# A two-phase attention and gated-product kernel: the joint between its phases is re-ordered, the rows before their second norm lose a shift, and a Gram matrix is computed as a triangle

## The chip, the core and the metric

The kernel runs on one core of a Trainium2 chip. The metric is device time in microseconds (us): the median of the runs before is 2426.33 us (three runs, 2426.27 to 2426.43). Four engines compute beside each other, each with its own queue of instructions that it takes in order: TensorE (PE; its weight loads are listed as PEld), VectorE (DVE), ScalarE (ACT) and GpSimd (POOL). SyncE (SP) issues most DMAs, also in order; ACT and POOL issue some.

## The reference, cut to what matters

The input x is 4 x 2048 rows of 512 numbers, all in float32.

```python
x = x + _layernorm(attn(_layernorm(x)))     # attention, causal, one head of 512
x = x + _layernorm(ffn(_layernorm(x)))

def attn(x):
    q, k, v = relu(x @ Wq + bq), relu(x @ Wk + bk), relu(x @ Wv + bv)
    e = q k^T / sqrt(512) - 10000 * causal
    return relu(softmax(e) @ v @ Wo + bo)

def _gated_bottleneck(x2d, conv_w, ...):    # twice, "so" and "si"
    xc = einsum('ngf,gf->ng', x2d.reshape(n, 128, 4), conv_w) + conv_b
    mean, var = over all n = 8192 rows      # one pair for each of 128 features
    xa = gelu((xc - mean) * rsqrt(var + eps) * gamma + beta)
    return xa @ lin_w.T + lin_b             # 512 logits of each row

def ffn(x):
    score_out = softmax(_gated_bottleneck(x, so...))   # the 32 largest of each row are kept
    out_branch = (x @ weight) at these 32 columns, times their scores
    score_in = softmax(_gated_bottleneck(x, si...))    # again the 32 largest
    in_branch = (x at these 32 columns, times their scores) @ weight
    return out_branch + in_branch + bias
```

The mean and variance of the features go over all rows, so no row can pass the second bottleneck before the last row's features exist. That cuts the kernel into two phases.

## The kernel before, in words

Rows are worked on in 16 groups of 512 (`NGRP`, four per sequence), each of four tiles of 128 rows (`TPG`). Phase 1 (`phase1`) computes attention and the features; phase 2 (`phase2`) the gated products. Both exist a second time with `every_key=True`, for inputs whose scores could be too large; whether that second pass runs is decided at the end from a bound (`compare`, L179), and it does not run in what is measured here.

**Phase 1.** `steps` (L906) goes over the groups. For each it does projections and earlier groups' scores as seven products instead of eight (class `Seven`; their PE rows are L555), its own scores (`score_tile`, L673), the maxima over keys, then `fold` (L707, four transposes, PE row L711), `diagonals` (L720: one DVE reduction, L717, and four scalings, L725), `spread` (L727, PE row L730), `weights` (L732: for each key tile a DVE subtraction and an ACT exponential, with row sums on POOL) and the attention products (`attend`, L768, PE row L773). A float32 matmul call shows as two MATMUL rows.

The order on PE, DVE and POOL is written by hand (`tc.manual_schedule`): the order of the calls is the order of the instructions, within each phase. A small planner, `Pace`, does it for DVE: work that DVE has to do is handed over as generators that yield how long each piece takes, `pace.pe(us)` says that PE was given so much work, and the planner emits as many DVE pieces as fit beside it; `pace.flush(job)` emits a job to its end, `pace.drain()` all. The order on ACT and SP in phase 1 is set by the framework, which simulates the program and may mix work of both phases on an engine.

`chain` (L796) is such a job, one for each tile of 128 rows, behind that tile's attention product. `attended` (L782) takes the product out of PSUM on DVE (L788) and through a Relu on ACT (L789). Then `row_norm` (L139) measures the row on DVE (L142, L144, L146), with an inverse square root on POOL (`inv_sqrt`, L137). With m and r, the residual row x is shifted on ACT by -m*r (L806), and DVE forms x1 = a*r + that (L809). x1 is stored, measured by a second `row_norm`, normed (L816) and stored, and DVE forms the features `xg` of both branches: two products with the convolution weights (L222) and two reductions (L824). In groups 0 to 14 further transposes and stores follow; features return by DMA as columns (`fetch_features`, L837), where a DVE statistic of 512 columns (L281) goes into `bn_all`. In the last group `features` (L843) transposes each tile's `xg` on PE (L847) and copies it into `xc` on ACT (L849), and behind the last tile come the two statistics of 512 columns (L851).

**The Gram product.** In the last group there is no next group to project, and its PE time is filled with `bound` (L861): the 512 x 512 product of the query weights with themselves, four blocks of 128 rows (d = 0 to 3), each over four row blocks c, that is 16 calls or 32 MATMUL rows at L869 and, for each d, one ACT Square with a sum (L877). It is a generator too: each `next(filler)` in `steps` emits half a block. Block 0 lies around `A.p7`, block 1 behind `A.p4` and ahead of `fold`, block 2 between `fold` and `spread`, the first half of block 3 ahead of the attention products and its second half at the end, between the features of tiles 1 and 2.

**The joint.** `phase2` (L1137) opens its pools where phase 1's lie; each of its tiles waits for those tiles of phase 1 whose memory it takes. It loads the Gelu table (`warm`, L1154), aggregates the statistics (L1159) to a scale and an offset for each feature (`bn_a2`, `bn_b2`: L1161 to L1170, with one POOL power), loads the weights `wf` by one DMA on SP (L97) and the bias by one on POOL (L90). It transposes the rows of tiles 0 and 1 (L164, copies L165), does half of tile 0's ungated product (`product`, L1311: four calls over c, 512 columns each), then the Gelu of the first 128 columns (`activate`, L1200), tile 0's logits (`logits`, L1223 and L1225), and the product's other half. `xnT` of every tile comes from the pool `wk2`.

**Phase 2's loop** takes one tile of 128 rows per turn: eight MAX8 and eight MATCH_REPLACE8 on DVE for the two branches (L1232, L1240, L1243), exponentials on ACT, masks and sums on POOL, two products on PE. In turn 1 it also does tile 1's ungated product:

```python
if it == 1:
    logits(nxt)
    n.full = product(n.xnT)
```

Of the kernel before, what the change touches and what calls it, by code (L numbers as in the profile page):

```python
# [39 lines left out]
P = 128  # L40
GT = 512
# [12 lines left out]
def sandwich_kernel(ctx: ExitStack, tc: tile.TileContext, io: dict, out: bass.AP):  # L54
# [52 lines left out]
    bn_all = const.tile([P, 2, NGRP, nc.vector.BN_STATS_DIM], F32, name="bn_all")  # L107
# [71 lines left out]
    def compare(ps):  # L179
# [5 lines left out]
        nc.vector.scalar_tensor_tensor(q4, tot[:, 0:1], float(D * D), q4, ALU.mult, ALU.add)  # L185
# [8 lines left out]


    def phase1(every_key):
# [15 lines left out]
        xgp = enter("xgp", TPG)  # L212
# [64 lines left out]
        pace = Pace()  # L277

# [5 lines left out]
        def load(b, g, queues=(nc.sync,)):  # L284
# [3 lines left out]
            n.x, n.ahead = [], []  # L288
# [507 lines left out]
        def chain(n, t):  # L796
# [5 lines left out]
            yield 1.0, (0.55,)  # L802

            shift = sm.tile([P, 1], F32, name="shift")
            combine(shift, m, r, ALU.mult, -1.0)
            nc.scalar.activation(xr, xr, AF.Identity, bias=shift)  # L806
            yield 0.2, 1.2
            x1 = two.tile([P, D], F32, name="x1")
            nc.vector.scalar_tensor_tensor(x1, a, r, xr, ALU.mult, ALU.add)  # L809
# [3 lines left out]
            m, r = row_norm(sm, x1, "x1")  # L813
            yield 1.75, (0.55,)
            xn2 = ap.tile([P, D], F32, name="a")
            nc.vector.tensor_scalar(xn2, x1, m, r, ALU.subtract, ALU.mult)  # L816
            store.dma_start(xn2_d[n.i][t * P : (t + 1) * P, :], xn2)
            yield 0.55, 0.0
            n.xg[t] = xg = xgp.tile([P, 2, P], F32, name="xg")
# [22 lines left out]

        def features(n, t):  # L843
# [4 lines left out]
            for j, br in enumerate(branches):  # L848
                nc.scalar.copy(xc[br][:, t * P : (t + 1) * P], ps[:, j, :])  # L849
                if t == TPG - 1:  # L850
                    nc.vector.bn_stats(bn[br][:, n.i, :], xc[br])  # L851
# [9 lines left out]
        def bound():  # L861
# [4 lines left out]
            for d in range(NC):  # L866
                ps = ps_mm.tile([P, GT], F32, name="mm")
                for c in range(NC):
                    nc.tensor.matmul(  # L869
                        ps, lhsT=w[c][1][:, d * P : (d + 1) * P], rhs=w[c][1], start=(c == 0), stop=(c == NC - 1)  # L870
                    )
                    if c % 2:
                        pace.pe(1.72)
# [3 lines left out]
                nc.scalar.activation(sqr, ps, AF.Square, accum_out=squared[:, 0, d : d + 1])  # L877
# [28 lines left out]
        def steps(n, ahead):  # L906
# [3 lines left out]
            for j in range(NGRP):  # L910
# [129 lines left out]
                if last:  # L1040
                    pace.drain()
                    features(n, 0)
                    features(n, 1)
                    next(filler)
                    features(n, 2)
                    features(n, TPG - 1)
                    break
# [25 lines left out]
        if every_key:  # L1073
            bo = broadcast(wp, "L0_attn_bo")
            for b in range(B):
# [11 lines left out]
                for g in range(GB):  # L1087
# [12 lines left out]
                    for t in range(TPG):  # L1100
# [3 lines left out]
                        if n.i == NGRP - 1:  # L1104
                            features(n, t)
                    if n.i < NGRP - 1:
                        fetch_features(n.i)
                        pace.drain()
        else:
# [24 lines left out]
        p1.close()  # L1134

# [364 lines left out]
```

## Time and profile before

| what | us |
|---|---|
| median of three runs | 2426.33 |
| profiled execution, its own time | 2428.16 |
| its span, first to last instruction | 2426.3 |
| PE busy in the span | 2376.5 (98%) |
| DVE busy | 1791.3 (74%) |
| ACT busy | 1119.3 (46%) |
| POOL busy | 925.5 (38%) |
| last attention product ends (PE) | about 1743.8 |
| first MAX8 of phase 2 starts (DVE) | 1761.35 |

The page gives busy time of each engine, its share in 40 equal slices of the span (a digit is tenths), and the granted TensorE clock. A line of the order of time gives start, duration, engine, line, operation and what it writes and reads; in brackets how long the engine was idle before it and what ended the wait. A line of the waits gives who waited for whom, the total, how often, and the longest. Time of an engine that is not the bound costs nothing by itself.

### The profile page before, as it was taken

The numbers are of one execution on the slowest core, as the hardware profiler recorded it, in microseconds if no ns is written. First come the engines' busy times: TensorE is split into PE (matmuls) and PEld (weight loads), VectorE is DVE, ScalarE is ACT, GpSimd is POOL, SyncE is SP. The second block draws the span as 40 slices with busy tenths as digits, with TensorE's granted clock in tenths as the row PEclk, the third lists the DMA queues.
The fourth block names the chain that finished last, engine by engine and source line by source line (L and its number), as shares of the span: only waits on it lengthen the run. The fifth ranks groups of instructions, "written<-read, shape, count | busy, mean of one in ns | idle before, by whom it ended". The sixth has DMA issues, their size and how long they took to land.

```text
span 2426.3 us, 29523 instructions
## 1 busy us (share of the span) xinstructions
PE 2376.5 (98%) x8418; PEld 1529.0 (63%) x8418; DVE 1791.3 (74%) x3877; ACT 1119.3 (46%) x2352; POOL 925.5 (38%) x875
## 2 busy tenths in 40 slices
PE   8999999999999999999999999999899999999997
PEld 3776858587685858768585776857334444444443
DVE  2587775558866555886655588655599999999997
ACT  2333423233342333334223333322268888888886
POOL 1012210311221031122103112110369999999997
PEclk9999999999999999999999999999999999999999
DMA  6587756567775556876565677633334445444441
GB/s 217 182 238 209 214 163 171 144 182 231 216 205 165 169 142 183 225 223 202 166 171 138 184 216 217 199 114 95 104 85 103 113 113 122 122 113 122 113 122 54
DMA packets 594736, 392.19 MB, mean 162 GB/s; under 512 B 393090, under 2 KB 460162, under 8 KB 594564
## 3 DMA queue, kind: packets, MB, share of 16 engines
q1 hardware_dynamic: 590932, 386.53, 57.8%
q10 hardware_dynamic: 3312, 2.63, 0.4%
q8 instruction: 70, 1.15, 0.2%
q0 software_dynamic: 320, 1.05, 0.1%
q14 instruction: 102, 0.84, 0.1%
HBM read 275.26 MB, written 114.82 MB: 161 GB/s over the span
## 4 chain that ended last, share of the span: by engine, by line
PE 76%; DVE 12%; ACT 4%; issue 4%; POOL 2%; DMA 1%; SPq 0%; POOLq 0%; ACTq 0%
PE acc L555 24%; PE acc L773 19%; PE mm L555 17%; PE mm L673 5%; PE mm L1311 4%; DVE m_si L1232 3%; DVE m_so L1232 2%; PE mm L408 2%; DVE rest_so L1240 2%; DVE rest_si L1240 2%; PE lg L1225 1%; DVE rest_si L1243 1%; DVE rest_so L1243 1%; PE tp L164 1%; PE mm L657 1%
## 5 line engine op out<-in xcount | busy, mean ns | idle before, releaser
L773 PE MATMUL acc<-vo,st 128*128 128x512 f32 x1088 | 475.9, 593 | 0.0
L773 PEld LDWEIGHTS acc<-vo,st 128*128 128x128 f32 x1088 | 205.3, 190 | 239.8 <-issue 234.6
L1311 PE MATMUL mm<-w_L_ffn_weight,xsT 128*128 128x512 f32 x512 | 231.2, 594 | 2.9 <-ACT xsT L165 1.6
L1311 PE MATMUL mm<-w_L_ffn_weight,xnT 128*128 128x512 f32 x512 | 232.2, 596 | 0.0
L137 POOL TENSOR_TENSOR rs_a<-ve_a,neg_half 128x1 f32<-128x1 f32 x64 | 38.4, 600 | 489.1 <-DVE ve_a L146 483.1
L1311 PEld LDWEIGHTS mm<-w_L_ffn_weight,xsT 128*128 128x128 f32 x512 | 97.5, 191 | 125.6 <-issue 115.6
L1311 PEld LDWEIGHTS mm<-w_L_ffn_weight,xnT 128*128 128x128 f32 x512 | 97.9, 192 | 122.6 <-issue 115.4
L137 POOL TENSOR_TENSOR rstd_x<-var_x,neg_half 128x4 f32<-128x4 f32 (+1 forms) x19 | 17.8, 936 | 403.3 <-DVE var_x L310 399.1
L555 PE MATMUL mm<-xnT,wb 128*128 128x256 f32 x720 | 170.1, 379 | 0.0
L555 PE MATMUL acc<-T,wb 128*128 128x256 f32 x720 | 170.1, 379 | 0.0
L743 POOL TENSOR_TENSOR mxsum<-mxsum,st 128x512 f32<-128x512 f32 (+2 forms) x144 | 162.8, 1131 | 14.7 <-ACT st L739 4.3
L555 PE MATMUL acc<-xnT,wb 128*128 128x256 f32 x720 | 165.2, 379 | 0.0
L555 PEld LDWEIGHTS acc<-T,wb 128*128 128x128 f32 x720 | 136.8, 190 | 25.0 <-issue 6.7
L555 PEld LDWEIGHTS acc<-xnT,wb 128*128 128x128 f32 x720 | 136.8, 190 | 25.0 <-issue 6.5
L555 PEld LDWEIGHTS mm<-xnT,wb 128*128 128x128 f32 x720 | 135.3, 190 | 24.0 <-issue 7.2
L673 PE MATMUL mm<-qT,kT 128*128 128x128 f32 (+3 forms) x512 | 148.5, 433 | 0.0
L574 ACT COPY cp<-mm 128x512 f32<-128x512 f32 x72 | 42.2, 586 | 203.6 <-PE mm L555 200.0
L222 DVE SCALAR_TENSOR_TENSOR mxsum<-mxsum,st 128x512 f32<-128x512 f32 (+2 forms) x144 | 86.4, 600 | 65.9 <-ACT st L601 61.3
L1232 DVE MAX8 m_si<-rest_si 128x8 f32<-128x512 f32 x192 | 130.1, 678 | 0.1
L1232 DVE MAX8 m_so<-rest_so 128x8 f32<-128x512 f32 x192 | 128.6, 670 | 0.1
L1240 DVE MATCH_REPLACE8 rest_si<-m_si,rest_si 128x512 f32<-128x512 f32 x192 | 128.5, 669 | 0.0
L1240 DVE MATCH_REPLACE8 rest_so<-m_so,rest_so 128x512 f32<-128x512 f32 x192 | 128.5, 669 | 0.0
(243 smaller groups left out, 4918.5 us busy)
## 6 DMA issues: line engine op xcount, KB each, us to landing
wb<-keys SPq DMA_DIRECT2D x168, 256.0 KB, 3.0
x<-x SPq DMA_DIRECT2D x124, 256.0 KB, 3.0
xr<-in_L_attn_x_dram SPq DMA_DIRECT2D x64, 256.0 KB, 3.6
xn<-xn SPq DMA_DIRECT2D x64, 256.0 KB, 2.8
out_dram<-h SPq DMA_DIRECT2D x64, 256.0 KB, 2.0
xt<-in_L_attn_x_dram SPq DMA_DIRECT2D x62, 256.0 KB, 3.5
wb<-Z_v SPq DMA_DIRECT2D x60, 256.0 KB, 2.9
wb<-Z_q SPq DMA_DIRECT2D x60, 256.0 KB, 3.1
```

What stands on the lines that cost most here:

```text
L137: nc.gpsimd.tensor_tensor(dst, src, neg_half[:, : src.shape[1]], ALU.pow)
L222: nc.vector.scalar_tensor_tensor(out, a, factor, b, ALU.mult, op)
L408: nc.tensor.matmul(ps, lhsT=w[c][1][:, d * P : (d + 1) * P], rhs=xnT[:, c, :], start=(c == 0), stop=(c == NC - 1))
L555: nc.tensor.matmul(ps[:, d * H : (d + 1) * H], lhsT=left[:, c, d * P : (d + 1) * P], rhs=right[:, c, :], start=(new and c + d == 0), stop= ...
L574: nc.scalar.copy(t, ps)
L673: nc.tensor.matmul(ps[:, off:], lhsT=kT[:, c, k : k + P], rhs=n.qT[:, c, off:], start=(c == 0), stop=(c == NC - 1),)
L743: nc.gpsimd.tensor_tensor(n.sum[:, off:], n.sum[:, off:], w, ALU.add)
L773: nc.tensor.matmul(acc, lhsT=n.st[kt][:, t * P : (t + 1) * P], rhs=vos[kt // TPG][:, kt % TPG, :], start=(kt == 0), stop=(kt == nk - 1),)
L1232: nc.vector.max(n.m8[br], n.rest[br] if k else n.lg[br])
L1240: nc.vector.match_replace(n.rest[br], n.m8[br], n.rest[br], -LOWEST)
L1243: nc.vector.match_replace(n.rest[br], n.m8[br], n.lg[br], -LOWEST)
L1311: nc.tensor.matmul(ps, lhsT=lhsT[:, c, :], rhs=wf[:, c, :], start=(c == 0), stop=(c == NC - 1))
```

## The change

Five edits.

1. **Triangle.** Block d of the Gram product takes only columns from d*128 on, so 512, 384, 256 and 128 of them; the planner is told 0.43 us times (4 - d) for half a block, and the bound counts the sum twice.
2. **Rows without the shift.** DVE forms y = a*r + x directly; the shift -m*r is added by ACT afterwards, and only for the row that is stored as x1. The second norm's moments and the normed row are taken from y, whose normed row is the same.
3. **Moments in parts.** In the last group the statistics of `xc` are taken of 384 columns, inside the last chain (`n.early`: one branch behind each `row_norm`), and of the last 128 columns in phase 2, straight from the transposes' PSUM; `bn_all` has one record more.
4. **Order of the joint.** The chains of tiles 0 to 2 are flushed, their features transposed, the Gram's last half emitted, and then the last chain. The last tile's features are transposed in phase 2, behind the whole ungated product of tile 0; aggregates, scale and offset follow there. Tile 1's ungated product lies in halves around tile 0's logits, and is gone from turn 1.
5. **Where tiles lie.** `wf` and `xnT` get pools of their own, next to the bottom of phase 2's memory; the last tile's `xg` gets a pool outside phase 1, and `bn_mv` is among the constants.

```diff
         def chain(n, t):
             m, r = row_norm(sm, a, "a")
             yield 1.0, (0.55,)
+            if n.early:
+                n.early.pop(0)()
+
+            y = two.tile([P, D], F32, name="x1")
+            nc.vector.scalar_tensor_tensor(y, a, r, xr, ALU.mult, ALU.add)
+            yield 0.75, 0.0
             shift = sm.tile([P, 1], F32, name="shift")
             combine(shift, m, r, ALU.mult, -1.0)
-            nc.scalar.activation(xr, xr, AF.Identity, bias=shift)
-            yield 0.2, 1.2
-            x1 = two.tile([P, D], F32, name="x1")
-            nc.vector.scalar_tensor_tensor(x1, a, r, xr, ALU.mult, ALU.add)
+            m, r = row_norm(sm, y, "x1")
+            x1 = xr
+            nc.scalar.activation(x1, y, AF.Identity, bias=shift)
             store = nc.scalar if final else nc.sync
             store.dma_start(x1_d[n.i][t * P : (t + 1) * P, :], x1)
-            m, r = row_norm(sm, x1, "x1")
-            yield 1.75, (0.55,)
+            yield 1.2, (0.55,)
+            if n.early:
+                n.early.pop(0)()
             xn2 = ap.tile([P, D], F32, name="a")
-            nc.vector.tensor_scalar(xn2, x1, m, r, ALU.subtract, ALU.mult)
+            nc.vector.tensor_scalar(xn2, y, m, r, ALU.subtract, ALU.mult)
...
+        def moments_of(br, i, src):
+            nc.vector.bn_stats(bn[br][:, i, :], src)
+
+        def first_moments(n, br):
+            moments_of(br, n.i, xc[br][:, : GT - P])
...
         def bound():
+                cols = slice(d * P, D)
                 for c in range(NC):
                     nc.tensor.matmul(
-                        ps, lhsT=w[c][1][:, d * P : (d + 1) * P], rhs=w[c][1], start=(c == 0), stop=(c == NC - 1)
+                        ps[:, cols],
+                        lhsT=w[c][1][:, d * P : (d + 1) * P],
+                        rhs=w[c][1][:, cols],
+                        start=(c == 0),
+                        stop=(c == NC - 1),
                     )
                     if c % 2:
-                        pace.pe(1.72)
+                        pace.pe(0.43 * (NC - d))
...
                 if last:
+                    pace.flush(*behind[:-1])
+                    for t in range(TPG - 1):
+                        features(n, t)
+                    next(filler)
+                    n.early = [(lambda br=br: first_moments(n, br)) for br in branches]
                     pace.drain()
-                    features(n, 0)
-                    features(n, 1)
-                    next(filler)
-                    features(n, 2)
-                    features(n, TPG - 1)
+                    ends.append(n.xg[TPG - 1])
                     break
...
         wp = enter("wp2", 1)
+        wfp = enter("wf2", 1)
+        xtp = enter("xt2", 3)
...
-        mv = wp.tile([P, 2, nc.vector.BN_AGGR_DIM], F32, name="bnmv")
-        for j, br in enumerate(branches):
-            nc.vector.bn_aggr(mv[:, j, :], bn[br].rearrange("p n s -> p (n s)"))
-        (scale and offset from it)
-        wf = matrix(wp, "L0_ffn_weight")
+        wf = matrix(wfp, "L0_ffn_weight")
...
-        tiles[0].full = product(tiles[0].xnT, part=range(2))
+        tiles[0].full = product(tiles[0].xnT)
+
+        for j, br in enumerate(branches):
+            tp = ps_tp.tile([P, NC, P], F32, name="tp")
+            nc.tensor.transpose(tp[:, j, :], xg[:, j, :], ident)
+            nc.vector.bn_stats(bn[br][:, NGRP, :], tp[:, j, :])
+            nc.vector.bn_aggr(bn_mv[:, j, :], bn[br].rearrange("p n s -> p (n s)"))
+            nc.scalar.copy(xc[br][:, GT - P :], tp[:, j, :])
+        (scale and offset from bn_mv)
+        tiles[1].full = product(tiles[1].xnT, part=range(2))
         activate(xa[0], slice(0, P))
         logits(tiles[0])
-        product(tiles[0].xnT, tiles[0].full, range(2, NC))
+        product(tiles[1].xnT, tiles[1].full, range(2, NC))
         activate(xa[0], slice(P, GT))
...
                 if it == 1:
                     logits(nxt)
-                    n.full = product(n.xnT)
```

## The prediction

> **What bounds the kernel now.** I read the page's busy shares first, then busy time by stage, the chain of waits, the waits around the seam, and the order of time there. On the page:
>
> ```profile
> PE   8999999999999999999999999999899999999997
> DVE  2587775558866555886655588655599999999997
> PEclk9999999999999999999999999999999999999999
> ```
>
> PE is full through phase 1, DVE through phase 2. Busy time in five stretches (stretch, length, then PE, PEld, DVE, ACT, POOL busy, granted clock, DMA share, GB/s) separates the joint from both:
>
> ```profile
> 0.00:1640.00 1640.00, 1629.96 (x6383) 1186.72 (x6384) 1077.30 (x2197) 545.89 (x1074) 288.55 (x324) 1.00 0.66 188
> 1640.00:1693.00 53.00, 53.00 (x220) 40.95 (x219) 22.76 (x48) 10.72 (x24) 0.10 (x1) 1.00 0.38 97
> 1744.00:1761.00 17.00, 10.09 (x27) 4.22 (x25) 9.88 (x24) 7.99 (x20) 2.55 (x7) 0.66 0.86 231
> 1761.00:2403.00 642.00, 624.25 (x1645) 270.63 (x1644) 641.48 (x1531) 532.21 (x1190) 602.91 (x515) 0.99 0.45 109
> ```
>
> Between 1761 and 2403 us DVE idles 0.5 us, so whatever brings its first MAX8 forward brings the end forward by as much. Before 1744 PE does not idle, so there only PE work or a wait that takes its place counts. In the 17 us between, neither is full: latency decides. The chain of waits shows where the Gram product stands in the last group:
>
> ```profile
> 1683.23 3.43 PE mm L869 x8
> 1686.66 0.44 PE tp L711 x4
> 1687.10 3.44 PE mm L869 x8
> 1690.53 0.86 PE mm L730 x2
> ```
>
> and the waits from 1640 to 1760 tell how much later PE came than its consumers:
>
> ```profile
> DVE fold L717 <- PE tp L711: 2.0, 1, 2.0
> DVE st L738 <- PE mm L730: 2.7, 1, 2.7
> ACT pr L877 <- DVE xg L824: 4.3, 1, 4.3
> ```
>
> In order of time, the joint, the last tile's chain and what follows it:
>
> ```profile
> 1743.82 0.75 DVE L788 SCALAR_TENSOR_TENSOR cp<-acc,rsum,r_L_attn_bo 128x512 f32<-128x512 f32 x1 [2.59 <-PE acc L773]
> 1747.33 0.72 ACT L806 ACTIVATE xr<-xr,shift 128x512 f32<-128x512 f32 x1 [0.47 <-DVE shift L222]
> 1748.08 0.75 DVE L809 SCALAR_TENSOR_TENSOR x<-cp,rs_a,xr 128x512 f32<-128x512 f32 x1 [0.79 <-ACT xr L806]
> 1753.25 0.69 DVE L824 TENSOR_REDUCE xg<-pr 128x128 f32<-128x512 f32 x1
> 1754.80 0.69 DVE L851 BATCH_NORM_STATS2 bn_all<-xc_so 128x6 f32<-128x512 f32 x1 [0.86 <-ACT xc_so L849]
> 1756.01 1.02 DVE L1159 BATCH_NORM_AGGREGATE bnmv<-bn_all 128x2 f32<-128x96 f32 x2
> 1758.69 0.49 ACT L1200 ACTIVATE xc_si<-xc_si,bnb,bna 128x128 f32<-128x128 f32 x1 [3.27 <-DVE bnb L1170]
> 1761.35 0.70 DVE L1232 MAX8 m_si<-lg 128x8 f32<-128x512 f32 x1 [2.75 <-PE lg L1225]
> ```
>
> From PE's last attention product to the first MAX8 is one chain of DVE, ACT, POOL and PE, 17.5 us long.
>
> **Triangle Gram.** The matmul rows stand 0.429 us apart at 512 columns, 0.322 at 384, 0.216 at 256 and 0.112 at 128 (the Gram, score and projection rows). Eight rows of d=1 fall from 3.43 to 2.58 us, of d=2 from 3.44 to 1.73, four of d=3 from 1.72 to 0.45; d=0 stays. What was hidden must be looked at each time. After d=1 the fold needs the maxima, whose last DVE row ends at 1685.16; PE would be there at 1683.06+2.58=1685.64, so PE still comes last: the fold gains 0.86. After d=2 the spread needs the diagonals: reduce and four scalings end at 1688.74, 0.86 earlier now, 1687.88; PE is free at 1686.08+1.73=1687.81. So DVE comes last by 0.07 and the spread starts at 1687.95 instead of 1690.37: 2.42 us gained, 1 us of the shortening lost to the diagonals. The half of d=3 before the attention gains nothing more, because the first exponential (spread to weight load 2.46 us, as in the trace) is late next: PE idles about 1 us. The transfers of the last features landed well before (their last issue is at 1664.66, their use at 1700.2), POOL's row sums keep their distance. **−2.42.** Bounds: −0.86 (only d=1) and −2.6.
>
> **Unshifted rows.** The chain's ACT pass L806 no longer stands between the inverse root and L809. Now: shift at 1747.13, ACT 1747.33, L809 1748.08, statistics 1748.87. After: the product at 1747.13, 0.75 long, statistics at 1747.92; the shift (0.15) overlaps its end. **−0.95** in the last tile. The ACT pass runs beside the statistics, and the store on ACT's queue (SP's in groups 0 to 14) goes out behind it, some 0.75 us later against the row; key blocks queue behind it on SP, with 13 of them (each 1.72 us of PE) in the ring. In those groups PE is the bound and gains nothing, except perhaps the four gaps of 0.26 to 0.39 us ahead of L555, where DVE finished a chain step first; I take 0, between −1.3 (all gone) and +1.3 (as many new ones).
>
> **Moments in parts.** Now, from xg's end at 1753.94: PE transposes, ACT copies, two statistics of 512 columns, two aggregates, end 1757.03: 3.09 us. After: 384 columns of each branch are measured in the two waits for POOL in the last chain (idle 0.66 and 0.67; price 0.56, from the 384-wide L222 row of 557 ns; 0.55 fits if tile 2's copies are done, which needs ACT to place them ahead of the Gelu table's 1.28 us). Behind xg stay two statistics of 128 columns (0.29 each, the 128-wide L222 row) and two aggregates (0.54 each with 17 records for 16): 1.66, plus 0.1 of starts, and the transposes of one branch lie beside the other's statistics: 1.79. **−1.3**; bounds −1.5 and 0 (a copy late by 0.6 in each wait).
>
> **First product ahead.** Moved: eight rows of tile 0's product before the last transposes, four of tile 1's behind them, the weight matrix's DMA (its row: issue 1744.60, 6.73 us to landing) to an earlier place on SP, whose queue is idle from 1664.66 to 1724.80; the bias broadcast and three memsets on POOL (0.6 and 0.12 each) ahead of the coefficients, in POOL's idle time. The product's other operand, xnT, is copied by ACT. Now that copy waits until 1753.30, behind L877 and the stores; L877 waited for the tile that L824 freed. After, L877 has a tile freed by tile 2's chain, and the copy should come behind the table load, about 1747.6 to 1748.2 on before's clock: eight rows of 0.429 end by 1751.7, before xg's first half is needed (1753.0). On the path nothing; 0.9 us of cover, beyond which each us costs one.
>
> What it brings is PE's clock. Now PE idles 5.7 us from 1747.03 and the granted share falls from 1.00 to 0.50 at 1749.5, until 1763.0: the first logits rows stand 0.853 apart, not 0.429. After, idle pieces are about 2 us each. A gap of 1.26 us at 1774 held the clock, one of 3.98 at 1779 lost it; mine lies nearer the first. At full clock the two rows to the first MAX8 cost 0.85 less, and the pipe behind them 0.1: **−0.95**, bounds −1.0 and +0.8 (tile 1's four rows at 0.853 end behind the Gelu and push the logits).
>
> A rule that speaks against this: the Trainium skill, "TensorE: Matmul & The Clock Gate", Part 4 "PE-mode transpose", says that a transpose doesn't count as PE work the way a matmul does. The trace agrees: the share fell at 1749.5, though eight transposes ran until 1747. By that rule my first gap is 3.0 us, from the Gram's end to the product, and by the same page's advice ("Why this matters for your kernels": no idle gaps over about 3 us) it is a coin's throw; the sum by it would be −3.7 to −5.0.
>
> **The sum:** 2.42+0.95+1.3+0.95 = 5.6 us. Steady tiles of phase 2 and the tail after 2403 have the same instructions: 0. The profiled execution took 2428.16: span 2426.3 and 1.9 around it; the median of the runs is 2426.33, 1.8 below. Span 2420.7, and 2420.7 for the median. 0.2% (4.85 us) is about what a measurement of this kernel can tell from no change, and the sum lies just over it.
>
> **Rivals.**
> - The clock falls in the first gap. For: eight transposes and 2 us of nothing. Against: dense work on both sides. The product takes up to 6.8 us for 3.4, ends by 1753.4 to 1754.7, and the last transposes start 0.7 to 2 us late: gain 3.7 to 5.0, time 2421.3 to 2422.7.
> - The change doesn't do what it says: the copy or the weights come late as now, because ACT is in order and has the two stores of the last chain (issued 1748.86 and 1751.21) ahead of it, or SP issues the weights no earlier. The product then ends near 1754.4 to 1755, 2 us into the path, at half clock more: gain 1 to 3.5, 2422.8 to 2425.3. Against: both waits seen now have their causes removed.
> - Slower: DVE's order in groups 0 to 14. The chain's steps are cut differently, and a step before an eviction stalls PE, as four times now for 0.26 to 0.39 us. It decides when new gaps exceed 5.6 us (15 gaps of 0.39); two in each of 15 groups, 11.7 us, give 2432.4. Against: 1640 us with 2.9 us of gaps, and a DVE one third idle.
>
> **Chances.** All as summed 0.52; clock falls 0.24; operands late 0.15; DVE's order 0.09, of which slower by over 0.2% is 0.05. Faster by over 0.2%: 0.45 of the first case (its own range 2419.2 to 2421.9) and 0.06 of the second, 0.51; slower 0.05; same 0.44. To leave out 2 in 10, the range reaches from 2419.0 (all four gaps gone too) to 2425.0, most of the third case.
>
> **What the profile after would show.** Right: the fold 0.9 and the first attention product 2.4 us earlier; no ACT row between inverse root and row product; DVE's statistics of 384 columns inside POOL's waits; weights landed by 1700; a granted clock of 1.00 through the joint; first MAX8 near 1755.7. Wrong: 0.853 between product rows, a wait of the last transposes for that product, the statistics waiting for ACT's copies, or new gaps ahead of L555.

## The result, and the profile after

The changed kernel takes 2423.12 us (median of 20 runs, 2421.82 to 2424.20) against 2427.35 us for the kernel before in runs beside them (20 runs, 2425.57 to 2428.70). The ratio is 0.9983, with a 95% interval of 0.9977 to 0.9989: 4.2 us, or 0.17%, are gone. The time lies inside the predicted range, the gain 1.4 us short of the predicted 5.6 and just under the bound of 0.2%. (The kernel before ran 1.0 us above the three runs that the prediction had to go by, so the predicted time itself is off by 2.4.) The profiled execution took 2423.45 us, its span 2421.7.

The same views as before, of the changed kernel. First the page's 40 slices:

```profile
PE   8999999999999999999999999999989999999997
DVE  2588675558866565887656678655599999999997
PEclk9999999999999999999999999999999999999999
```

Nothing has changed places: PE bounds phase 1, DVE phase 2. Busy time by stage (stretch, length, then PE, PEld, DVE, ACT, POOL, granted clock, DMA share, GB/s):

```profile
0.00:1640.00 1640.00, 1629.29 (x6381) 1185.38 (x6382) 1074.41 (x2196) 544.84 (x1074) 292.65 (x324) 1.00 0.66 188
1640.00:1691.00 51.00, 50.02 (x221) 40.99 (x219) 23.05 (x49) 10.15 (x24) 0.00 (x0) 1.00 0.45 127
1742.00:1756.20 14.20, 9.91 (x38) 4.83 (x36) 10.24 (x26) 7.25 (x20) 2.61 (x7) 1.00 0.53 163
1756.20:2398.00 641.80, 620.17 (x1636) 268.67 (x1636) 641.61 (x1531) 532.37 (x1191) 602.72 (x515) 0.99 0.45 109
```

The third line is the joint (14.37 us long, 17.73 before, by the count below); PE's clock in it is 1.00, 0.66 before. Ahead of the last attention PE now idles 1.0 us of 51, where it was full. In phase 2 DVE idles 0.2 us of 642. The chain of waits at the Gram product:

```profile
1683.73 2.58 PE mm L886 x8
1686.75 1.73 PE mm L886 x8
1688.54 1.11 PE mm L736 x2
1689.67 0.70 DVE st L744
1690.39 0.64 ACT st L745
1691.07 23.44 PE acc L779 x54
```

Block 1 takes 2.58 us for 3.43 and block 2 1.73 for 3.44, as worked out. The subtraction and the exponential of the first key tile have come onto the chain behind the spread (0.70 and 0.64 us). The waits from 1640 to 1757 say the same, who waits for whom, total, times, longest:

```profile
DVE fold L723 <- PE tp L717: 1.1, 1, 1.1
DVE st L744 <- PE mm L736: 1.3, 1, 1.3
PE acc L779 <- ACT st L745: 1.0, 1, 1.0
```

The consumers of PE wait 1.1 and 1.3 us where they waited 2.0 and 2.7, and PE itself now waits 1.0 for ACT. The joint in order of time:

```profile
1742.06 0.75 DVE L794 SCALAR_TENSOR_TENSOR cp<-acc,rsum,r_L_attn_bo 128x512 f32<-128x512 f32 x1 [4.64 <-PE acc L779]
1744.62 0.55 DVE L855 BATCH_NORM_STATS2 bn_all<-xc_so 128x6 f32<-128x384 f32 x1
1745.38 0.75 DVE L813 SCALAR_TENSOR_TENSOR x<-cp,rs_a,xr 128x512 f32<-128x512 f32 x1 [0.21 <-POOL rs_a L139]
1746.19 3.70 PE L1325 MATMUL mm<-w_L_ffn_weight,xnT 128*128 128x512 f32 x8 [1.67 <-ACT xnT L167]
1746.23 0.72 ACT L819 ACTIVATE xr<-x,shift 128x512 f32<-128x512 f32 x1
1750.07 0.30 PE L1338 MATMUL tp<-ident,xg 128*128 128x128 f32 x1 [0.18 <-DVE xg L835]
1750.56 0.69 DVE L835 TENSOR_REDUCE xg<-pr 128x128 f32<-128x512 f32 x1
1752.29 0.62 DVE L1340 BATCH_NORM_AGGREGATE bn_mv<-bn_all 128x2 f32<-128x102 f32 x1
1754.51 0.49 ACT L1214 ACTIVATE xc_si<-xc_si,bnb,bna 128x128 f32<-128x128 f32 x1 [1.96 <-DVE bnb L1354]
1756.22 0.70 DVE L1246 MAX8 m_si<-lg 128x8 f32<-128x512 f32 x1 [1.74 <-PE lg L1239]
```

Between inverse root and row product no ACT row is left (the shift's pass runs at 1746.23, behind it); a statistic of 384 columns lies in POOL's wait, which leaves DVE 0.21 us idle of 0.66; the eight rows of the product take 3.70 us, full clock, and PE waits for the features, not the features for PE.

Counted from the end of the last attention product (taken as the start of PE's next row, 1743.62 us before and 1741.86 now), in us:

| | before | after | gained up to here |
|---|---|---|---|
| row product (L809, now L813) starts | 4.46 | 3.52 | 0.94 |
| last feature reduction (L824, now L835) ends | 10.32 | 9.39 | 0.93 |
| last aggregate ends | 13.41 | 11.05 | 2.36 |
| first Gelu starts | 15.07 | 12.66 | 2.41 |
| first MAX8 starts | 17.73 | 14.37 | 3.36 |

So by these two traces the rows gave 0.93, the moments 1.43 and the clock 0.95. The whole span of the two profiled executions can be accounted for in the same way. (PE runs at half clock from its first projection row for some us, rows 0.853 us apart, and loses half of that time: the second row. Its gaps are pauses of over 0.15 us.)

| piece of the span | before | after | difference |
|---|---|---|---|
| first projection row starts (PE) | 13.04 | 13.35 | +0.31 |
| half of the time from there to the full clock | 2.92 | 2.70 | -0.22 |
| PE's gaps in groups 0 to 14 | 1.31 | 1.67 | +0.36 |
| all else up to the last group's first attention row | 1675.68 | 1673.35 | -2.33 |
| the last group's attention products | 50.68 | 50.78 | +0.10 |
| joint | 17.73 | 14.37 | -3.36 |
| first MAX8 to the end of DVE's last row | 657.17 | 657.17 | 0.00 |
| from there to the end of the span | 7.76 | 8.26 | +0.50 |
| span | 2426.3 | 2421.7 | -4.6 |

The first two rows differ from execution to execution of any kernel here (12.62 to 13.35 and 1.5 to 2.9). With them taken out, the fourth row is a constant: 1675.68 to 1675.72 in the three traces with the whole Gram, 1673.32 to 1673.36 in the ten with the triangle and the attention as it was. That makes differences of 0.1 us readable from single traces.

Beside 0.10 us in the attention and the start, two rows run against the change, the gaps and the end. The prediction had both at 0, and the experiments go after them.

### The profile page after: what moved, and what is told of

The parts are those of the page before. It is cut to its first block, busy times and chain, and to the rows that moved or that the text cites. A ratio compares the mean times of both kernels' runs of the same rounds, so it can differ in the third digit from the quotient of the medians.

```text
span 2421.7 us, 29446 instructions
## 1 busy us (share of the span) xinstructions
PE 2368.4 (98%) x8418; PEld 1526.3 (63%) x8418; DVE 1788.8 (74%) x3879; ACT 1117.2 (46%) x2352; POOL 929.8 (38%) x875
## 3 DMA queue, kind: packets, MB, share of 16 engines
q10 hardware_dynamic: 3312, 2.63, 0.3%
## 4 chain that ended last, share of the span: by engine, by line
PE 73%; DVE 15%; ACT 4%; issue 4%; POOL 2%; DMA 1%; SPq 0%; POOLq 0%; ACTq 0%; DVEq 0%
PE acc L561 24%; PE acc L779 18%; PE mm L561 18%; PE mm L679 6%; DVE m_si L1246 4%; DVE m_so L1246 3%; DVE rest_so L1254 2%; DVE rest_si L1254 2%; PE mm L1325 2%; PE mm L414 2%; DVE rest_si L1257 1%; DVE rest_so L1257 1%; PE lg L1239 1%; PE mm L663 1%; PE mm L736 1%
## 5 line engine op out<-in xcount | busy, mean ns | idle before, releaser
L139 POOL TENSOR_TENSOR rs_a<-ve_a,neg_half 128x1 f32<-128x1 f32 x64 | 44.5, 696 | 417.1 <-DVE ve_a L148 416.2
```

The lines of the kernel that those rows point to most:

```text
L139: nc.gpsimd.tensor_tensor(dst, src, neg_half[:, : src.shape[1]], ALU.pow)
```

## The experiments

The theory to test: four steps give 2.4, 0.95, 1.3 and 0.95 us, and the shortfall lies outside of them, in the last stretch of the span. The rivals: that the change came off the path in one of the four (a clock that falls, operands that come late), or that phase 1 lost time to DVE's order.

**The changed kernel again,** on the chip of the next three, as their yardstick.

> The changed kernel once more, beside the runs of the kernel before on this chip. Theory (the steps add up): against the kernel before the first attention product of the last group 1.9 us earlier, the joint (from the end of the last attention product to the first MAX8) 14.4 us for 17.7, together 5.1 us to the first MAX8, and what lies behind it equal but for the landing of the last stores; the time 4.2 to 5.6 us shorter. Rival (the trace flatters it, and 4 us is all there is): the same positions in the trace, but the median again 4.2 us or less below.

2422.92 us (2421.64 to 2424.05), ratio 0.9981 (0.9972 to 0.9990) against 2427.32 for the kernel before. Joint 14.36, gaps 1.68, the end after DVE's last row 8.62 us. The accounting above repeats. The gain by medians is 4.4 us, between what was expected and its rival, so it decides nothing between them.

**Triangle alone,** in the kernel before (with it go the Square, of the same columns, and a factor of 2 in the bound):

```diff
+                cols = slice(d * P, D)
-                    nc.tensor.matmul(ps, lhsT=w[c][1][:, d * P : (d + 1) * P], rhs=w[c][1], ...)
+                    nc.tensor.matmul(ps[:, cols], lhsT=..., rhs=w[c][1][:, cols], ...)
-                        pace.pe(1.72)
+                        pace.pe(0.43 * (NC - d))
```

> The kernel before with the triangle Gram alone. Theory: first attention product 2.4 us earlier than before, 1 us of PE idle ahead of it, the joint unchanged at 17.7 us, the whole 2.4 us shorter (ratio 0.9990). Rival (a wait takes the place of the Gram's rows): the spread and the first exponential come as late as now, first attention product 0 to 0.9 us earlier, the whole within 1 us of before.

2424.19 us (2423.24 to 2426.05), ratio 0.9989 (0.9980 to 0.9998). The fourth row of the accounting falls by 2.36, from 1675.68 to 1673.32, and the attention takes 0.10 more. The joint, which this edit does not touch, is 16.78 us instead of 17.73: its half-clock stretch began at 1745.7 and ended at 1756.0, ahead of the logits' rows, so these ran at full clock. That is luck of position: the product starts 10.64 us after the attention in both kernels, but here it fills a window of the clock (1752.5 to 1756.0, PE busy 3.42 of 3.42 us; on these windows more below), behind which the full clock came back, and in the kernel before it lies across two (2.63 and 3.03 of 3.41), and the clock came back behind the next. The triangle's own share is 2.26 us.

**Everything but the triangle:** the changed kernel with whole blocks of 512 columns (the diff above, reversed).

> The changed kernel with the whole Gram product. Theory: 2.4 us longer than the changed kernel, so some 2 to 3 us shorter than before; the last half block of the Gram (1.72 us for 0.45) moves the transposes of tiles 0 and 1 by 1.27 us, which the Gelu table's load covers, so the joint stays at 14.4 us. Rival (the joint needs the short Gram): the product starts 1.3 us later, its end passes the last features, and the joint is 0.5 to 1.3 us longer.

2425.24 us (2424.65 to 2426.41), ratio 0.9992 (0.9983 to 1.0001): 2.3 us above the changed kernel, and by the accounting 2.36 less 0.10. Both directions agree. The joint is 14.54 us although the product starts 1.29 us later (5.63 us after the attention's end instead of 4.34), because ACT's order, set by the framework, puts the copy of xnT behind the chain's own ACT pass here. The clock stayed at 1.00, and those 1.29 us cost 0.17: the cover of the product is about 1.1 us as long as PE runs at full clock.

**Shifted rows again** in all groups, the rest as changed:

```diff
-            y = two.tile([P, D], F32, name="x1")
-            nc.vector.scalar_tensor_tensor(y, a, r, xr, ALU.mult, ALU.add)
-            yield 0.75, 0.0
             combine(shift, m, r, ALU.mult, -1.0)
-            m, r = row_norm(sm, y, "x1")
-            x1 = xr
-            nc.scalar.activation(x1, y, AF.Identity, bias=shift)
+            nc.scalar.activation(xr, xr, AF.Identity, bias=shift)
+            yield 0.2, 1.2
+            x1 = two.tile([P, D], F32, name="x1")
+            nc.vector.scalar_tensor_tensor(x1, a, r, xr, ALU.mult, ALU.add)
             store.dma_start(...)
-            yield 1.2, (0.55,)
+            m, r = row_norm(sm, x1, "x1")
+            yield 1.75, (0.55,)
...
```

> The changed kernel with the shift on ACT ahead of the row product again, in all groups. Theory: the joint 0.95 us longer (15.3 us), and the PE gaps of groups 0 to 14 go back to 0.26 to 0.39 us, 1.3 us in all for 1.7, so the whole is 0.5 us longer than the changed kernel. Rival (the planner's cut of the chain matters more than the shift): gaps change by over 1 us in sum in either direction and decide the total.

2421.75 us (2421.03 to 2422.34), ratio 0.9977 (0.9968 to 0.9986): faster than the changed kernel by 1.2 us, though a step is undone that gains. The joint is longer as it should be, 15.23 us: the row product starts at 4.48 again and the first MAX8 0.87 later. But the gaps in groups 0 to 14 are back at 1.32 us, and the end behind DVE's last row takes 7.06 us instead of 8.26 to 8.62. So two effects that the prediction had at 0 outweigh a step of 0.9. (Expected were 0.5 us more, or as rival gaps that change by over 1 us; neither came.) For the gaps, the waits in the first 1640 us, of the kernel before:

```profile
PE acc L555 <- DVE vo L607: 1.3, 4, 0.4
```

of the changed kernel:

```profile
PE acc L561 <- DVE st L609: 1.1, 3, 0.4
PE acc L561 <- DVE qT L613: 0.5, 1, 0.5
```

and of this one:

```profile
PE acc L561 <- DVE vo L613: 1.3, 4, 0.4
```

The four gaps of before are here under the same statement's new number, of the same sizes (0.27 to 0.39 us). In the changed kernel none is left where it was, near 358, 785, 1211 and 1638 us. Three of 0.37 to 0.38 us lie near 588, 1014 and 1441, behind another eviction, and one of 0.55 near 191. The order of time there, of the changed kernel:

```profile
186.65 5.82 POOL L749 TENSOR_TENSOR mxsum<-mxsum,st 128x512 f32<-128x512 f32 x5 [0.26 <-ACT st L745]
186.94 1.64 DVE L227 SCALAR_TENSOR_TENSOR pr<-a,convw_so 128x512 f32<-128x512 f32 x1
189.22 1.04 DVE L227 SCALAR_TENSOR_TENSOR pr<-a,convw_si 128x512 f32<-128x512 f32 x1
190.19 0.68 DVE L613 TENSOR_TENSOR qT<-acc,xr 128x512 f32<-128x512 f32 x1
190.92 1.99 PE L561 MATMUL acc<-T,wb 128*128 128x256 f32 x8 [0.55 <-DVE qT L613]
```

and of the kernel before:

```profile
187.09 1.65 DVE L222 SCALAR_TENSOR_TENSOR pr<-a,convw_so 128x512 f32<-128x512 f32 x1
189.38 0.68 DVE L607 TENSOR_TENSOR qT<-acc,xr 128x512 f32<-128x512 f32 x1
189.97 0.68 DVE L222 SCALAR_TENSOR_TENSOR pr<-a,convw_si 128x512 f32<-128x512 f32 x1
```

In the kernel before, the eviction for which PE waits stands between DVE's two products with the convolution weights; the new cut of the chain puts it behind both. The products take 0.65 to 0.69 us elsewhere. Here, beside POOL's row sums, the first takes 1.64 us, in the kernel before too, where it costs PE nothing; the second takes 1.04, some 0.37 of the gap's 0.55 by these rows. Running beside the sums is not enough to explain that: the second product of the kernel before does so as well and takes 0.68. What stretches them stays open. In the last group the same rows run with POOL idle.

**Moments whole:** no early statistics; behind the last transposes an ACT copy, then statistics of 512 columns, then both aggregates.

```diff
-                    n.early = [(lambda br=br: first_moments(n, br)) for br in branches]
...
-            nc.vector.bn_stats(bn[br][:, NGRP, :], tp[:, j, :])
-            nc.vector.bn_aggr(bn_mv[:, j, :], bn[br].rearrange("p n s -> p (n s)"))
             nc.scalar.copy(xc[br][:, GT - P :], tp[:, j, :])
+            nc.vector.bn_stats(bn[br][:, NGRP - 1, :], xc[br])
+        for j, br in enumerate(branches):
+            nc.vector.bn_aggr(bn_mv[:, j, :], bn[br].rearrange("p n s -> p (n s)"))
```

> The changed kernel with the last group's statistics taken whole, 512 columns of each branch behind the last copies, and no early part. Theory: the joint 1.3 to 1.4 us longer, 15.8 us, from two copies and two statistics of 0.69 us in place of two of 0.29. Rival (the early parts cost as much in the chain as they save behind it): the chain from the last product out of PSUM to the last feature is 0.5 us or more shorter without them, and the joint at most 0.9 us longer.

One run: 2425.24 us, 2428.05 for the kernel before beside it. Joint 17.24 us, 2.87 more than changed. This is more than the moments alone, and the trace says why: the copy of xnT again came at 5.02, the clock fell to 0.50 from 1746.9 to 1750.3 and once more from 1757.1 to 1760.5, the product took 5.40 us, and the last transposes began 10.87 us after the attention instead of 8.2 and 9.5. So it does not measure the moments cleanly, and no other run takes them alone: their 1.43 is from the two traces' rows. It shows something else: the cover that made a late product cheap at full clock is gone at half clock.

**The product behind:** tile 0's product in halves around its logits, as before, with all else as changed.

```diff
-        tiles[0].full = product(tiles[0].xnT)
...
-        tiles[1].full = product(tiles[1].xnT, part=range(2))
+        tiles[0].full = product(tiles[0].xnT, part=range(2))
...
-        product(tiles[1].xnT, tiles[1].full, range(2, NC))
+        product(tiles[0].xnT, tiles[0].full, range(2, NC))
```

> The changed kernel with the first ungated product behind the last features again (half of it, then the logits, then the rest; tile 1's in turn 1), all else as changed. Theory: PE idles some 5.5 us, the granted clock falls to 0.50 inside the joint, the first logits rows stand 0.853 us apart for 0.429, and the joint is 0.95 to 1.8 us longer. Rival (the clock is not what the order brings): the clock stays at 1.00, or the rows stay at 0.429, and the joint is as long as in the changed kernel within 0.3 us.

One run: 2423.94 us. Joint 15.29 us, 0.92 more than changed. Of this, 0.12 is there at the first Gelu, where DVE takes the first branch's statistic ahead of the second reduction; the other 0.80 lies behind it, where the product's rows run at half clock. Busy time by windows of the clock, of this kernel:

```profile
1744.50:1747.90 3.40, 0.00 (x0) 0.00 (x0) 3.07 (x8) 1.97 (x5) 0.55 (x1) 1.00 0.29 106
1747.90:1751.31 3.41, 1.03 (x3) 0.79 (x4) 3.23 (x7) 0.27 (x1) 0.00 (x0) 0.50 0.49 119
1751.31:1754.72 3.41, 3.41 (x5) 0.80 (x4) 1.72 (x8) 1.22 (x4) 0.70 (x1) 0.50 0.90 311
```

A window in which PE did nothing, then two at half clock, in which four product rows take 3.62 us and hold up the logits. In the changed kernel the product ahead of the last features fills that empty window.

**The weights at the old place,** in the pool `wp2`:

```diff
-        wfp = enter("wf2", 1)
-        wf = matrix(wfp, "L0_ffn_weight")
+        wf = matrix(wp, "L0_ffn_weight")
```

> The changed kernel with the ungated product's weights in the pool at the bottom of phase 2's memory, as before, where the attention's output bias lay. Theory: their DMA is issued only behind the last product's way out of PSUM, near 1742.9 us, lands some 6.7 us later, and the product runs from 1749.6 to 1753 or later, so the last transposes wait for it: joint 2 to 4 us longer. Rival (hidden anyway): the DMA lands in 3 to 4 us now that nothing else is on the queues, the product ends before the last features, and the joint is at most 0.5 us longer.

One run: 2425.22 us. Joint 17.47 us, 3.1 more. In order of time, of this kernel:

```profile
1741.31 0.38 SPq L97 DMA_DIRECT2D w_L_ffn_weight<-in_L_ffn_weight_dram  x1
1747.05 5.11 PE L1324 MATMUL mm<-w_L_ffn_weight,xnT 128*128 128x512 f32 x8 [4.05 <-DMA w_L_ffn_weight<-in_L_ffn_weight_dram]
1752.00 0.38 PE L1337 MATMUL tp<-ident,xg 128*128 128x128 f32 x2
```

The DMA is issued 1 us after the attention's end instead of 76 us ahead of it (at 1665.69 in the changed kernel). PE waits 4.05 us for it; the clock falls within that wait, the product takes 5.11 us, and both transposes wait for the product.

**xnT at the old place,** in the pool `wk2`:

```diff
-        xtp = enter("xt2", 3)
-            n.xnT = xtp.tile([P, NC, P], F32, name="xnT")
+            n.xnT = wk.tile([P, NC, P], F32, name="xnT")
```

> The changed kernel with the transposed rows in the pool from which they came before. Theory: the first copy waits for a tile of the last chain, as before, and comes 2 us or more later, the product's end passes the last features and the joint is 1 to 3 us longer. Rival (it was the Square of the Gram that held ACT, waiting for a tile that the last features freed): the copy comes at the same time as in the changed kernel, joint unchanged within 0.2 us.

One run: 2425.00 us. Joint 19.27 us, 4.9 more, 1.5 longer than before the change. In order of time, of this kernel:

```profile
1747.10 0.33 ACTq L828 DMA_DIRECT2D xn<-a  x1
1747.47 1.07 ACT L167 COPY xnT<-tp 128x512 f32<-128x512 f32 x2 [1.92 <-DMA x<-xr]
1748.11 6.40 PE L1324 MATMUL mm<-w_L_ffn_weight,xnT 128*128 128x512 f32 x8 [4.99 <-ACT xnT L167]
```

The copy comes behind both stores of the last chain, PE waits 5 us, and eight rows take 6.40 us at half clock. That its time is no worse than the one above is due to the end of the span, 6.30 us here against 8.46 there. Without either place, then, the new order of the joint loses more than it gains: 17.47 and 19.27 us against 15.29 with the product behind.

**The end of the span.** The page has no row for it, since semaphore events are not counted. In the trace's records SyncE, behind the last store (0.03 us after the end of DVE's last row) and a compare-and-branch (0.42), has 24 records of closing events and drains, which fill the last 2 to 4 us. Their distances, in us after DVE's last row:

| kernel | first event | spacing of the next ones | longest pause | end |
|---|---|---|---|---|
| before | 4.51 | 0.06 to 0.10 | 1.04, after 15 events | 7.76 |
| changed | 4.07 | 0.06 to 0.10 | 2.03, after 3 events | 8.26 |
| shifted | 4.47 | 0.06 to 0.09 | 0.73, after 22 events | 7.06 |
| xnT at the old place | 4.12 | 0.06 to 0.09 | none | 6.30 |

(Near the end, one distance of 0.16 and a last one of up to 0.50 us are in every trace.) The same 24 records, with a pause of another size at another place, which goes with the kernel: after 3 events in both traces of the changed kernel, after 15 in the kernel before and with the triangle alone. That looks as if it depended on where the end lies in SyncE's program, and all these kernels have SyncE programs of different lengths. If so, instructions that are never executed must move it. The second phase 1 and 2, behind the bound's test, is such a place:

```diff
     with tc.If(is_small == 0):
         xg = phase1(every_key=True)
         with tc.manual_schedule(engines=ENGINES):
             phase2(True, xg)
+        for _ in range(24):
+            nc.sync.dma_start(sums_d["v", "Z1"][:, :P], ident)
```

**The changed kernel with its end moved:**

> The changed kernel with 24 small DMAs more on SP in the branch that is not executed, so that the end of SP's instructions lies elsewhere and nothing else differs. Theory (SP's closing events stand still for 1.9 to 2.0 us behind the third of them because of where they lie in SP's program): the pause goes, from the last VectorE row to the end of the span 6.3 us for 8.3 to 8.6, first MAX8 and joint unchanged, the median about 2421.0 us, 2 us below the changed kernel's. Rival (the pause belongs to the last stores or the semaphores): it stays, the median within 0.5 us of the changed kernel's 2422.9.

2420.77 us (2419.96 to 2421.17), ratio 0.9974 (0.9964 to 0.9984).

**The kernel before with its end moved,** by the same 24 lines:

> The kernel before with the same 24 DMAs in the branch that is not executed. Theory: its pause of 1.05 us goes as well, 6.7 us behind the last VectorE row for 7.8, the median about 2426.2 us; against it the changed kernel with its end moved is 5 us shorter, what the steps add up to. Rival: pause and median stay, 2427.3 us.

2426.15 us (2425.82 to 2427.16), ratio 0.9997 (0.9988 to 1.0006).

Both pauses are gone, and both ends take 6.74 us; the first event comes 4.57 us after DVE's last row and no distance is over 0.50. The medians fall by 2.35 us (2.15 against the changed kernel's second series) and by 1.16; the traces of the end account for 1.5 (1.9 by the second trace) and 1.0 of that. Gaps and joints are as they were (1.70 and 14.37; 1.32 and 17.72). The two kernels with equal ends are 5.38 us apart in their medians. By the accounting of their two traces, the first two rows left out, it is 5.2: 2.34 in the fourth row and 3.35 in the joint, less 0.10 in the attention, 0.38 in the gaps and 0.05 in phase 2. This is what the change gains when the ends are equal.

**Unshifted rows in the last group only:** the old order of the chain in groups 0 to 14 (`if final:` around the new one).

> The changed kernel with the rows unshifted in the last group alone, the old order in groups 0 to 14. Theory: PE's gaps of groups 0 to 14 are those of before, 1.3 us for 1.7, the joint 14.4 us as in the changed kernel, so 0.4 us less to the first MAX8; the end changes with where SP's last instructions come to lie. Rival (the gaps belong to another edit): 1.7 us of gaps as in the changed kernel.

One run: 2420.74 us. The gaps are 1.31 us, the joint 14.36, the end 6.49 without a pause. The 0.37 us come back in the groups, and the last tile keeps its gain. So the gaps are due to the new order of the chain and to nothing else in the change.

**All together:** the old order in groups 0 to 14, the moved end, and, because PE idles 1.0 us for the first exponential, the first key tile of the last group in two parts.

```diff
+                cuts = (0, P, GT) if kt == 0 and n.i == NGRP - 1 else (off, GT)
+                for c0, c1 in zip(cuts, cuts[1:]):
+                    part = n.st[kt][:, c0:c1]
+                    nc.vector.tensor_tensor(part, part, n.mb[:, c0:c1], ALU.subtract)
+                    nc.scalar.activation(part, part, AF.Exp, scale=scale)
```

> The changed kernel with the unshifted rows in the last group alone, the first key tile's weights of the last group in two column parts (128 and 384), and SP's end moved by the 24 unexecuted DMAs. Theory: gaps 0.4 us less, the first attention product of the last group 0.8 us earlier (PE idle 0.2 us ahead of it for 1.0), the pause at the end 2.0 us less: median about 2419.8 us, below the changed kernel and before. Rival (the framework places ACT's copy of the first rows behind the last chain's pass again, 1.3 us later, as with the whole Gram): joint 0.2 to 3 us longer, median 2420 to 2423 us.

2420.36 us (2419.67 to 2420.69), ratio 0.9972 (0.9961 to 0.9982): it beats both kernels, by 7.0 and about 2.7 us, and the changed kernel with its end moved by 0.4, about what the gaps give. Little of this is the parts: the first attention row comes 0.74 us earlier by the accounting (1672.61), but the attention then takes 51.31 us instead of 50.78. In order of time, of this kernel:

```profile
1688.18 1.13 PE L782 MATMUL acc<-vo,st 128*128 128x512 f32 x2 [0.28 <-ACT st L748]
1689.56 2.84 PE L782 MATMUL acc<-vo,st 128*128 128x512 f32 x6 [0.26 <-ACT st L748]
```

After two rows PE waits again, 0.26 us, for the next key tile's exponential. Net 0.2 us: ACT and DVE, not the first tile's size, set the pace there.

## Why the prediction was right or wrong

**Triangle, -2.42: right.** 2.36 to the attention (two pairs of traces), 2.26 to its end. The late step named for it, PE idle about 1 us for the first exponential, is there with 1.0.

**Unshifted rows, -0.95 in the last tile: right,** 0.93, and 0.87 when undone. **The 0 for groups 0 to 14 was wrong,** within its bounds: +0.36. It was argued from PE being the bound; but chain steps stand ahead of evictions for which PE waits, and the new cut put other steps ahead of other evictions, in one place a product that is stretched beside POOL's row sums.

**Moments, -1.3: right, a little small.** 3.09 us became 1.66, so -1.43. The aggregates took 0.61 to 0.62 us each where 0.54 was reckoned, but the first branch's transpose and statistic lie beside the second's reduction, which pays for that and for the 0.1 of starts. No run isolates the step.

**Clock, -0.95: right.** 0.95 in the two profiles; 0.80 behind the first Gelu, 0.92 in all, in the run with the product behind. The early places were needed: 3.1 and 4.9 us are lost without them. The rival priced late operands at up to 4.6 us of lost gain; one of the two runs went beyond, since copy, half clock and the waiting transposes add up. In the medians the clock step may be worth less than in its trace: with the old joint, traces showed 17.73 (twice) and 16.78 (once, in the kernel with only the triangle), depending on where the clock's windows fell.

**The cover of 0.9 us** was about right as a number (1.29 late cost 0.17 at full clock) and wrong in its reason. The product ends 8.03 us after the attention and the first half of the features 8.07, so towards the first half there is next to none; the path goes through the second half, 1.3 us later. I had taken the end of the second reduction for the first.

A rule had been weighed here. The Trainium skill, "TensorE: Matmul & The Clock Gate", Part 4 "PE-mode transpose", says that a transpose does not count as PE work the way a matmul does. The prediction read the kernel before as agreeing, but the window in which its clock was lost (1746.0 to 1749.4) was busy for only 0.30 of its time, transposes counted. The runs went the other way. The windows of the clock in the changed kernel:

```profile
1742.48:1745.90 3.42, 1.76 (x14) 1.52 (x14) 2.35 (x6) 3.39 (x12) 1.36 (x5) 1.00 0.31 69
1762.97:1766.38 3.41, 0.68 (x2) 0.00 (x0) 3.41 (x8) 0.93 (x2) 0.83 (x1) 1.00 0.74 128
```

In the first, PE is busy 1.76 us, and only the Gram's four rows (0.61) are no transposes; the clock held. In the second 0.68 us of plain matmul were busy, and the clock fell behind it, at 1766.4. If transposes had counted for nothing, the first window would have been the emptier one. The other traces agree. In seven (the five with this joint, the shifted rows and the product behind) the window at the head of the joint held the clock with 0.18 to 0.23 of its time in rows other than transposes. Windows without any transpose lost it with 0.20 to 0.36 of their time in such rows (0.36 with all together, 1760.1 to 1763.5). So these float32 transposes, done as matmuls against the identity, did count; no run varied them alone. The joint's clock was 1.00 in all five traces with this joint (the changed kernel twice, with its end moved, and the last two kernels). In these five the joint starts 2.5 to 3.3 us into a window of 3.41; whether the clock holds at other positions was not seen.

**The step that failed** is the sentence "Steady tiles of phase 2 and the tail after 2403 have the same instructions: 0." The steady tiles have: 657.17 us in both. The tail has the same instructions too, and takes 0.50 us more in one trace and 0.86 in the other, for a pause in SyncE's closing events whose length depends on where they lie in its program. Same instructions were taken for same time. The sum with what was measured: 2.26 + 0.93 + 1.43 + 0.95 - 0.36 - 0.50 to 0.86 = 4.3 to 4.7, less at times when the old joint's clock is lucky; the medians say 4.2 and 4.4. With equal ends 5.38 were measured, against 5.6 predicted. It was the tail and the gaps, both taken as 0, that brought the gain from over 0.2% to just under it.

**The rivals.** The clock did not fall in the first gap; the operands came in time (ACT's copy at 3.73 us, 4.0 to 4.6 had been read off); DVE's order in groups 0 to 14 did come into play, with a fifteenth of the 5.6 us that would have decided.

## What to carry to other kernels

In a stretch where latency decides, the terms of such a sum could be read here from the trace of before to 0.15 us, provided each is followed to the row that is late next; the operands of whatever is moved ahead (here a weight matrix and one ACT copy) decide whether the whole joint gains 3.4 us or loses 1.5. When the effect looked for is below 0.3%, the ends of the program count too: measure both kernels with the same pause, or none, before crediting a step or blaming it. And a chain that was cut anew gained here where it was the path, and lost where another engine was the bound: there it is better left in its old cut.

## What the runs showed of the hardware that was not expected

- **A pause at the end.** SyncE's closing events, 0.06 to 0.10 us apart, contain a pause of 0 to 2.1 us that goes with the position of the end in SyncE's program: instructions that are never executed removed it, for 1.16 and 2.15 to 2.35 us of the medians. That it is the loading of code is likely: the DMA records have packets of 8 KB on an instruction queue (q14) there, and in all nine traces with a pause one of them ends 1.04 to 1.22 us before SyncE goes on, whether the pause began after 2, 3, 15 or 22 events. But such a packet is there in the five traces without a pause too, and the records do not say whose code it carries; so it is not shown.
- **The clock moves on a grid that the program does not set.** Stretches at one clock lasted 3.4, 6.8, 10.2, 13.7 and 20.5 us, all multiples of 3.413, and the time from the first projection row to the full clock was 2.97 to 5.83 us in fourteen traces. The Trainium skill, "TensorE: Matmul & The Clock Gate", Part 1 "What's actually happening", gives a free-running window of 3413 ns; these durations agree. For a difference of 1 us it means that half of that start (1.5 to 2.9 us) is noise, and that a joint with idle PE can be 1 us longer or shorter by position alone.
- **How busy a window must be stayed open.** In the fourteen traces, windows with PE busy for up to 0.36 of the time lost the clock; the one above with 0.52 held it, and one of `xnT_late` (from 2409.0) with 0.46. But three windows lost it at 0.54 (weights late), 0.61 (unshifted rows in the last group only) and 0.63 (shifted rows, 1808.2 to 1811.7). All three have 0.6 us of bf16 rows on 3 partitions in them; other windows with such rows held it from 0.62 on. A rule by share alone does not fit, and whether such rows count for less was not tried.
- **ACT's order is not local.** The copy of xnT came 3.73, 4.35 or about 5.0 us after the attention's end depending on edits elsewhere (the chain's order; the Gram's width, the place of the statistics), because the framework orders ACT by its own simulation. At full clock that cost 0.17 us, at half clock it was part of 2.9.
